# Batch 0's rows in 32-partition transfers, transposes between the units ahead of it, and part of its projections and FFN moved into it

## The chip, the cores and the metric

The kernel is written in Bass for one Trainium2 chip and runs on one of its cores. A core has five engines with instruction streams of their own: TensorE (PE in the profile, with its weight loads as PEld), VectorE (DVE), ScalarE (ACT), GpSimd (POOL) and SyncE (SP), which only starts transfers here. Transfers are issued from SP, from ScalarE's queue (ACTq) and from GpSimd's queue (POOLq), and are carried out by 16 DMA engines. The metric is the time of one execution on the device in microseconds (us); less is better.

## The reference, cut to what matters

x is [16, 512, 128] in fp32: 16 batches of 512 tokens. Wq and Wk are [128, 128] (16 heads of 8), Wv is [128, 1024] (16 heads of 64), Wo is [1024, 128], and the three FFN weights are [128, 128].

```python
xn = (x - mean(x)) / sqrt(var(x) + 1e-5)            # over the last axis
# causal attention, 16 heads, d_k = 8, d_v = 64
q, k, v = heads(xn @ Wq), heads(xn @ Wk), heads(xn @ Wv)
scores = einsum('bhqd,bhkd->bhqk', q, k) / sqrt(8)
attn = softmax(where(causal, -inf, scores))
a = concat_heads(einsum('bhqk,bhkd->bhqd', attn, v)) @ Wo
# FFN on the same xn; prev is xn one token earlier (zeros for the first)
xr = mu_r * xn + (1 - mu_r) * prev
xk = mu_k * xn + (1 - mu_k) * prev
f = sigmoid(xr @ W_r.T) * (square(relu(xk @ W_k.T)) @ W_v.T)
out = x + a + f
```

## The kernel before, in words

**Rows of q and k.** q and k are kept in fp32, each split into a rounded high half and the rest (hi and lo), so that a product of short depth (8 dimensions, as hi, lo, hi of k against hi and lo of q, in 32 rows, with a row or more for statistics behind them) gives fp32 accuracy. project_qk makes the product for all heads with tokens in the free dimension, VectorE splits it (qh and ql, kh and kl), and the halves are written to DRAM: two blocks of 256 KB for q, three for k (hi, lo, hi). spread_qk reads them back in the layout of the matmuls: head pair p (two heads, u = 0 and 1, on partitions from 64u on) holds 32 rows of 512 elements of 2 KB each. One spread fills 16 partitions for several pairs: m = 0 or 1 chooses the lower or the upper 16 of the 32. make_qk reserves the tiles and fills the constant rows by GpSimd's transfers (k<-fill, q<-fill); batch b uses tile b % 2.

**Units.** The attention of one batch is cut into four groups of two head pairs, and each group into UNITS = 5 units, 20 units per batch (`per`), 320 in all, which are counted on through the batches as n. A group's rows go through two passes. In the row pass, rowscores puts q·k (tile sm) into PSUM, rowmask adds the mask, rowmax takes the negative row maximum on VectorE, and rowsum takes the exponential on ScalarE with the sum accumulated. After a group's five units the logarithm of the sums is subtracted from the maximum, transposed (turn_stats) and written into q's rows 33 and 34 by two GpSimd transfers per half (put_stats: q<-mh and q<-ml). In the second pass, scores makes the transposed product (tile sT) with these rows, weights takes its exponential (tile e), and weigh multiplies with v (tile av). The row pass of unit n + 11 is issued with the second pass of unit n: LEAD = 10 units are finished ahead. Units −11 to −1 therefore hold only row work, and are called the lead here; unit 0 issues the first scores.

**What else stands in a unit.** `at(n, f, ...)` puts a piece of other work into unit n, for the same batch or for the next two: layer norm (row_moments, deviation, normalise, transpose_xn), project_qk, spread_qk, project_v (eight products pv per batch of two matmuls each, each followed by a copy into v), mix_prev and mix, and the FFN: ffn_r (product pr) and ffn_exp (e_sig), ffn_sig (reciprocals), ffn_k (product pk), ffn_out (product pkv), then project_out (product po), and load_x. In a unit, unit_work's order is put_stats, rowscores, scores, rowmask, rowmax, rowsum, weights, the pieces, weigh, turn_stats. In unit_work and its pieces every engine keeps the order in which the program is written (the wrapper `_InOrder`, whose line is L44 in the profile: nearly all instructions show that line and are told apart by their tiles). Plain `nc.` calls, as in load_x, are not held to it.

**PSUM.** There are two sm tiles of two banks (ps_sm), one sT tile of two (ps_st), one bank for av (ps_av) and one for everything else (ps_m). m_tile gives out the last one; as long as the list `lent` is not empty (until n = −1) it rotates over ps_m, ps_av and ps_st, which nothing else uses yet.

**Before unit −11.** The program loads x of batches 0 and 1 on SP, the weights Wq, Wk, Wv, the three FFN weights and Wo on ScalarE's queue, sets up constants on GpSimd, normalises batch 0, projects its q (halves written from SP) and k (from ScalarE's queue), builds the mask operands (wide, id2, mask2), spreads pairs 0 and 1 (k on ScalarE's queue, q on SP), then pairs 2 and 3 (SP), transposes the FFN weights (wt), and normalises and projects q of batch 1. Pairs 4 to 7 are spread in units −8 to −5. All eight pv of batch 0 stand in units −10 to −1, pr in −2 and e_sig in −1:

```python
    for m, n in enumerate((0, 2, 3, 4, 5, 6, 7, 9)):
        at(first + n, project_v, 0, m // 2, m % 2)   # first = -LEAD
    at(first + 8, ffn_r, 0)
    at(first + 9, ffn_exp, 0)
    for c, n in enumerate((1, 2, 3, 3)):
        at(n, ffn_sig, 0, c)
    at(2, ffn_k, 0)
    at(4, ffn_out, 0)
```

Of the kernel before, what the change touches and what calls it, by code (L numbers as in the profile page):

```python
# [9 lines left out]
FP = mybir.dt.float32  # L10
# [7 lines left out]
P = 128  # L18
H = 16
DK = 8  # L20
DV = 64
NPAIR = H // 2
RS = 33
RA = 35
UNITS = 5
LEAD = 10
# [23 lines left out]
def attn_ffn_kernel(  # L50
# [27 lines left out]
    nc = tc.nc  # L78
    B, T, D = x.shape
    NB = T // P  # L80
    scale = 1.0 / math.sqrt(DK)

    const = ctx.enter_context(tc.tile_pool(name="const", bufs=1))
# [3 lines left out]
    one = ctx.enter_context(tc.tile_pool(name="one", bufs=1))  # L87
# [3 lines left out]
    dram = ctx.enter_context(tc.tile_pool(name="dram", bufs=2, space=bass.MemoryType.DRAM))  # L91
    ps_sm = ctx.enter_context(tc.tile_pool(name="ps_sm", bufs=2, space=PSUM))
    ps_st = ctx.enter_context(tc.tile_pool(name="ps_st", bufs=1, space=PSUM))
# [5 lines left out]
    pe, dve, act = _InOrder(tc, nc.tensor), _InOrder(tc, nc.vector), _InOrder(tc, nc.scalar)  # L99
    pool, sp = _InOrder(tc, nc.gpsimd), _InOrder(tc, nc.sync)  # L100
# [3 lines left out]
    def load_x(b):  # L104
        xs[b] = xp.tile([P, NB, D], FP, tag="x", name=f"x_{b}")
        nc.sync.dma_start(out=xs[b], in_=x[b].rearrange("(c p) d -> p c d", p=P))
# [4 lines left out]
    for name, w in (("wq", Wq), ("wk", Wk)):  # L111
        t = one.tile([P, H * DK], FP, tag=f"{name}_n", name=f"{name}_n")
# [1 line left out]
        wqk_n.append(t)  # L114
    wv = const.tile([P, H * DV], FP, tag="wv", name="wv")
    nc.scalar.dma_start(out=wv, in_=Wv)
    ffn_n = []
    for i, w in enumerate((W_r, W_k, W_v)):
        t = one.tile([P, D], FP, tag=f"ffn_n{i}", name=f"ffn_n{i}")
        nc.scalar.dma_start(out=t, in_=w)  # L120
        ffn_n.append(t)
    wo = const.tile([P, NPAIR, D], FP, tag="wo", name="wo")
    nc.scalar.dma_start(out=wo, in_=Wo.rearrange("(m p) d -> p m d", p=P))
    if B > 1:
        load_x(1)
    mus = const.tile([P, 2], FP, tag="mus", name="mus")
# [23 lines left out]
    lent = [0]  # L150

    def m_tile(name):
        n = lent[0] % 3 if lent else 0
        if lent:
            lent[0] += 1
        if n == 1:
            return ps_av.tile([P, T], FP, tag="av", name=name)
        if n == 2:
            return ps_st.tile([P, 2, 512], FP, tag="sT", name=name)[:, 0, :]
        return ps_m.tile([P, 512], FP, tag="m", name=name)  # L160

    xnTs, vs, ctxs, ffns, xmix = {}, {}, {}, {}, {}

# [18 lines left out]
    def row_moments(b, c):  # L182
        if c == 0:
            xs[b, "st"] = small.tile([P, NB, 6], FP, tag="st", name=f"st_{b}")
        dve.bn_stats(xs[b, "st"][:, c, :], xs[b][:, c, :])

    def deviation(b):
        st = xs.pop((b, "st"))
        mv = small.tile([P, NB, 2], FP, tag="mv", name=f"mv_{b}")
        for c in range(NB):  # L190
            dve.bn_aggr(mv[:, c, :], st[:, c, :])
        ve = small.tile([P, NB], FP, tag="ve", name=f"ve_{b}")
        dve.tensor_scalar(ve, mv[:, :, 1], EPS, None, ALU.add)
        rstd = small.tile([P, NB], FP, tag="rstd", name=f"rstd_{b}")
        pool.tensor_tensor(rstd, ve, neg_half, ALU.pow)
        xs[b, "mv"] = mv, rstd

    def normalise(b, c, engine=pool):
        if c == 0:
            xs[b, "n"] = small.tile([P, NB, D], FP, tag="xn", name=f"xn_{b}")  # L200
        mv, rstd = xs[b, "mv"]
        engine.tensor_scalar(
            xs[b, "n"][:, c, :], xs[b][:, c, :], mv[:, c, 0:1], rstd[:, c : c + 1],
            ALU.subtract, ALU.mult,
        )

    def transpose_xn(b):
        xn = xs.pop((b, "n"))
        pt = m_tile(f"xnTp_{b}")
        for c in range(NB):  # L210
            pe.transpose(pt[:, c * P : (c + 1) * P], xn[:, c, :], ident)

        xnT = big.tile([P, T + 1], FP, tag="xnT", name=f"xnT_{b}")
        pool.memset(xnT[:, 0:1], 0.0)
        dve.tensor_copy(xnT[:, 1 : T + 1], pt)
        xnTs[b] = xnT

    def project_qk(b, is_k, queue=sp):

        w, name = (wk, "k") if is_k else (wq, "q")  # L220
        pq = m_tile(f"p{name}_{b}")
        product(pq, w, xnTs[b][:, 1 : T + 1])
        hi = one.tile([P, T], FR, tag=f"{name}h", name=f"{name}h_{b}")
        lo = one.tile([P, T], FR, tag=f"{name}l", name=f"{name}l_{b}")
        dve.tensor_copy(hi, pq)
        dve.tensor_tensor(lo, pq, hi.bitcast(FP), ALU.subtract)

        blocks = (hi, lo, hi) if is_k else (hi, lo)
        d = dram.tile([len(blocks), P, T], FP, tag=name, name=f"{name}_{b}")
        for n, half in enumerate(blocks):  # L230
            queue.dma_start(out=d[n], in_=half.bitcast(FP))
        halves[b, name] = d.rearrange("n (d p u) t -> u (n d) p t", u=2, d=DK)

    def spread_qk(b, is_k, m, u, pairs, queue=sp):

        to, name = ((ks if is_k else qs)[b % 2].bitcast(FP), "k" if is_k else "q")
        first = DK * m if is_k else 0
        queue.dma_start(
            out=to[64 * u + 16 * m : 64 * u + 16 * m + 16, pairs],
            in_=halves[b, name][u][first : first + 16, pairs],  # L240
        )

    SPREAD = [(is_k, m, u) for m in range(2) for is_k in (False, True) for u in range(2)]

    def project_v(b, j, i):
        if j == 0 and i == 0:
            vs[b] = big.tile([P, NB, H * DV], FP, tag="v", name=f"v_{b}")
        pv = m_tile(f"pv_{b}_{j}_{i}")
        product(pv, xnTs[b][:, 1 + j * P : 1 + (j + 1) * P], wv[:, i * 512 : (i + 1) * 512])
        dve.tensor_copy(vs[b][:, j, i * 512 : (i + 1) * 512], pv)  # L250

    def mix_prev(b, i):
        prev = one.tile([P, T], FP, tag="prev", name=f"prev_{b}_{i}")
# [75 lines left out]

    def rowscores(b, g, t):  # L330
        q, k = qs[b % 2], ks[b % 2]
        sm = sms[b, g, t] = ps_sm.tile([P, 2, 512], FP, tag="sm", name=f"sm_{b}_{g}_{t}")
        for w, i, to in ROWS[t]:
            n = (i + 1) * P
            for u in range(2):
                s = slice(64 * u, 64 * u + RS)

                pe.matmul(
                    sm[:, u, to : to + n], q[s, 2 * g + w, i * P : n], k[s, 2 * g + w, :n],
                    start=(to == 0), stop=False,  # L340
                )
# [148 lines left out]
    def at(n, f, *args):  # L490
        todo.setdefault(n, []).append((f, args))
# [86 lines left out]
    def make_qk(i):  # L578
        q = const.tile([P, NPAIR, T], FR, tag=f"q{i}", name=f"q{i}")
        k = const.tile([P, NPAIR, T], FR, tag=f"k{i}", name=f"k{i}")  # L580
        for u in range(2):
            r = 64 * u + 32
            for to, value, n in ((q, 0, 1), (k, 1, 3)):
                pool.dma_start(
                    out=to[r : r + n].bitcast(FP),
                    in_=fill[0:n, value : value + 1, :].to_broadcast([n, NPAIR, T]),
                )
        qs.append(q)
        ks.append(k)


    make_qk(0)
    for c in range(NB):
        row_moments(0, c)
    deviation(0)
    for c in range(NB):
        normalise(0, c, dve)
    transpose_xn(0)
    project_qk(0, False)
    project_qk(0, True, act)  # L600

# [17 lines left out]
            dve.tensor_copy(to[half], wide[half, i, P * u : P * u + P])  # L621

    make_qk(1)
    for pairs in (slice(0, 2), slice(2, 4)):
        for is_k, m, u in SPREAD:
            spread_qk(0, is_k, m, u, pairs, act if is_k and pairs.stop == 2 else sp)

    ffn_w = const.tile([P, 3, D], FP, tag="ffn_w", name="ffn_w")
    wt = m_tile("wt")
    for i in range(3):  # L630
        pe.transpose(wt[:, i * D : (i + 1) * D], ffn_n[i], ident)
    dve.tensor_copy(ffn_w.rearrange("p i d -> p (i d)"), wt[:, 0 : 3 * D])


    omm = const.tile([P, 2], FP, tag="omm", name="omm")
    dve.tensor_scalar(omm, mus, -1.0, 1.0, ALU.mult, ALU.add)
    load_x(2)
    for c in range(NB):
        row_moments(1, c)
    deviation(1)  # L640
    for c in range(NB):
        normalise(1, c, dve)
    transpose_xn(1)
    project_qk(1, False)
    first = -LEAD
    at(first + 1, project_qk, 1, True)
    for m, part in enumerate(SPREAD):
        at(first + 2 + m // 2, spread_qk, 0, *part, slice(4, NPAIR))
    for m, n in enumerate((0, 2, 3, 4, 5, 6, 7, 9)):
        at(first + n, project_v, 0, m // 2, m % 2)  # L650
    for i in range(2):
        at(first - 1 + 5 * i, mix_prev, 0, i)
        at(first + 1 + 6 * i, mix, 0, i)
    at(first + 8, ffn_r, 0)
    at(first + 9, ffn_exp, 0)
    for c, n in enumerate((1, 2, 3, 3)):
        at(n, ffn_sig, 0, c)
    at(2, ffn_k, 0)
    at(4, ffn_out, 0)
    at(1, mix_prev, 1, 0)  # L660
    at(5, mix, 1, 0)
    for n in range(first - 1, B * per + 2):
# [38 lines left out]
```

## Time and profile before

| | us |
|---|---|
| median of 3 runs | 1011.81 (1010.26 to 1013.88) |
| profiled execution, in all | 1015.34 |
| its span, first to last instruction | 1013.6 |
| PE busy | 949.4 (94%) |
| ACT busy | 921.6 (91%) |
| DVE busy | 790.4 (78%) |
| POOL busy | 512.4 (51%) |
| mean granted TensorE clock | 0.975 |
| first row exponential (ACT sm) | 29.43 |
| first scores product (PE sT), unit 0 | 57.46 |
| first sT of batch 1 | 123.07 |

The profile is one execution, taken by the hardware profiler. Its page cuts the span into 40 slices of 25.3 us and shows the busy share of each engine in tenths, and the granted clock of TensorE (PEclk; 9 is 90% or more of full speed). Answers of the trace give the same for stretches of any length, single instructions with the idle time before them and what ended it, the sums of such waits, the chain of work that ended last, followed back from its end, and the transfers with the time from issue to landing. In the slices the first four differ from the rest: lower clock, and ScalarE starting late. A busy PE is not PE at full speed: the same product of two to four matmuls takes twice as long at a granted clock of 0.5.

### The profile page before, as it was taken

How to read it: one execution, taken by the hardware profiler on the slowest of the kernel's cores; microseconds unless marked ns; L12 is line 12 of the kernel's file. 1: busy time of each engine (PE TensorE's matmuls, PEld its weight loads, DVE VectorE, ACT ScalarE, POOL GpSimd, SP SyncE). 2: the span in 40 equal slices, each digit the busy share in tenths (PEclk: the TensorE clock that was granted, in tenths of full speed). 3: DMA queues.
4: the chain of work that ended last, by engine and by line, in shares of the span. 5: the costliest groups of instructions: out<-in, count | busy, mean ns of one | idle time of the engine just before them, and what ended most of it. 6: DMA issues, size and time to landing. Idle time of an engine off the chain costs nothing.

```text
span 1013.6 us, 22825 instructions
## 1 busy us (share of the span) xinstructions
PE 949.4 (94%) x8131; PEld 524.4 (52%) x8131; DVE 790.4 (78%) x1312; ACT 921.6 (91%) x2449; POOL 512.4 (51%) x959
## 2 busy tenths in 40 slices
PE   3888999999999999999999999999999999999997
PEld 1244464555546455554645555464555646455454
DVE  4777878787887878788787878878787887877641
ACT  0688999999999999999999999999999999999982
POOL 4146364554646455454645555464465546434431
PEclk8578999999999999999999999999999999999999
DMA  8730513535142353514235341423534131343000
GB/s 183 134 45 13 110 19 70 91 70 91 34 101 28 70 91 70 90 34 99 31 70 90 70 91 34 96 34 70 90 71 81 33 95 25 70 80 49 3 13 11
DMA packets 59968, 67.10 MB, mean 66 GB/s; under 512 B 12928, under 2 KB 33024, under 8 KB 59856
## 3 DMA queue, kind: packets, MB, share of 16 engines
q1 hardware_dynamic: 48688, 61.89, 32.4%
q10 hardware_dynamic: 2528, 2.43, 1.0%
q0 software_dynamic: 8640, 1.34, 1.0%
q8 instruction: 65, 1.06, 0.5%
q14 instruction: 47, 0.39, 0.1%
HBM read 39.13 MB, written 25.17 MB: 63 GB/s over the span
## 4 chain that ended last, share of the span: by engine, by line
ACT 55%; PE 27%; issue 8%; DVE 7%; DMA 2%; POOL 1%; ACTq 0%; POOLq 0%
ACT sm L44 37%; ACT e L44 17%; PE av L44 9%; PE po L44 5%; DVE negm L44 4%; PE sm L44 4%; PE pv L44 3%; PE sT L44 3%; PE xnTp L44 1%; PE pr L44 1%; DVE xnT L44 1%; DMA q<-ml 1%; DVE v L44 1%; DMA k<-k 1%; PE pk L44 1%
## 5 line engine op out<-in xcount | busy, mean ns | idle before, releaser
L44 ACT ACTIVATE sm<-sm,negm 128x384 f32<-128x384 f32 (+3 forms) x1024 | 513.0, 501 | 64.9 <-DMA k<-k 27.3
L44 DVE TENSOR_REDUCE negm<-sm 128x2 f32<-128x768 f32 (+3 forms) x448 | 397.9, 912 | 101.3 <-PE sm L44 99.2
L44 POOL TENSOR_SCALAR_AFFINE_SELECT e<-e 128x256 f32<-128x256 f32 x512 | 200.5, 410 | 432.4 <-ACT e L44 432.3
L44 PE MATMUL av<-e,v 128*64 128x512 f32 (+3 forms) x2048 | 336.5, 438 | 2.4 <-DVE ctx L44 2.4
L44 ACT ACTIVATE e<-sT 128x1024 f32<-128x1024 f32 x320 | 324.1, 1013 | 14.1 <-PE sT L44 14.1
L44 PEld LDWEIGHTS av<-e,v 128*64 128x64 f32 x2048 | 139.7, 137 | 161.6 <-issue 129.6
L44 ACT ACTIVATION_READ_ACCUMULATOR sm<-sm,negm 128x1 f32 x1024 | 200.5, 196 | 0.0
L44 PE MATMUL sm<-k,q 33*128 33x384 f32 (+3 forms) x1024 | 164.8, 378 | 7.4 <-ACT sm L44 5.4
L44 PE MATMUL sT<-q,k 35*128 35x512 f32 (+3 forms) x1024 | 147.7, 335 | 16.5 <-ACT e L44 13.0
L44 PEld LDWEIGHTS sm<-k,q 33*128 33x128 f32 x1024 | 83.6, 188 | 151.8 <-ACT e L44 82.0
L44 PE MATMUL pv<-wv,xnT 128*64 128x512 f32 x512 | 142.3, 633 | 12.6 <-DVE kl L44 5.8
L44 PE MATMUL po<-wo,ctx 128*64 128x128 f32 x2048 | 133.2, 277 | 2.9 <-DVE ctx L44 1.6
L44 PEld LDWEIGHTS po<-wo,ctx 128*64 128x64 f32 x2048 | 109.8, 137 | 15.4 <-DVE v L44 2.6
L44 PEld LDWEIGHTS sT<-q,k 35*128 35x128 f32 x1024 | 91.2, 187 | 45.9 <-ACT e L44 40.0
L44 DVE COPY v<-pv 128x512 f32<-128x512 f32 x128 | 87.6, 684 | 23.2 <-PE pv L44 19.7
L44 DVE COPY ctx<-av 128x512 f32<-128x512 f32 x128 | 87.1, 680 | 12.7 <-PE av L44 12.6
L44 PE MATMUL sm<-mask,id 64*128 64x256 bf16 (+1 forms) x640 | 91.0, 265 | 0.0
L44 POOL DMA_DIRECT2D q<-mh x128 | 69.8, 548 | 24.9 <-DVE mh L44 12.8
L44 POOL DMA_DIRECT2D q<-ml x128 | 65.8, 519 | 0.0
L44 DVE RECIPROCAL sig<-e_sig 128x128 f32<-128x128 f32 x64 | 60.1, 940 | 0.0
L44 POOL TENSOR_SCALAR prev<-xnT,omm 128x512 f32<-128x512 f32 x32 | 50.0, 1564 | 16.2 <-DVE xmix L44 16.2
L44 PEld LDWEIGHTS <-id 64*128 64x128 bf16 x640 | 36.3, 95 | 24.8 <-issue 10.5
(63 smaller groups left out, 571.1 us busy)
## 6 DMA issues: line engine op xcount, KB each, us to landing
q<-q SPq DMA_DIRECT2D x124, 128.0 KB, 4.9
k<-k SPq DMA_DIRECT2D x124, 128.0 KB, 4.7
k<-kh SPq DMA_DIRECT2D x30, 256.0 KB, 2.6
x<-in_L_attn_x_dram SPq DMA_DIRECT2D x16, 256.0 KB, 6.5
q<-qh SPq DMA_DIRECT2D x16, 256.0 KB, 2.0
q<-ql SPq DMA_DIRECT2D x16, 256.0 KB, 2.1
out_dram<-o SPq DMA_DIRECT2D x16, 256.0 KB, 2.8
k<-kl SPq DMA_DIRECT2D x15, 256.0 KB, 2.0
```

Source lines behind the costliest of these rows:

```text
L44: return self._tc.keep_in_program_order(f(*args, **kwargs))
```

## The change

The diff does these things.

- **Halves of k.** The high half of k is written to its two blocks in DRAM by one transfer with a repeated source, instead of two.
- **Spreads of batch 0, pairs 0 to 3.** spread_pair replaces spread_qk there: each transfer fills 32 partitions of one pair (64 KB) where it filled 16 partitions of two pairs (64 KB). The source is walked as two blocks of 16 rows: for q the same 16 rows twice (step 0), for k the second block 8 rows further on. The order is pair by pair; k of pairs 0 and 1 is on ScalarE's queue, the rest on SP.
- **Loads.** The three FFN weights are loaded from SP behind these spreads, and Wo from SP; both were on ScalarE's queue at the start.
- **Third row tile.** Row units 2, 5 and 8 of batch 0 use the ps_st tile; m_tile rotates over two places, not three.
- **TensorE kept busy.** keep_awake(n) issues n transposes of the identity into a spare tile: 32 at the start, 4 behind the transposes of xn, 8 in each of the units −9 to −1.
- **Moved work.** The first half of v's products (pv with i = 0) stands ahead of the spreads, with copies on ScalarE; the second half (i = 1) in units 0, 1, 2 and 4. pr moves from unit −2 to 2, e_sig from −1 to 3, the reciprocals from units 1, 2, 3, 3 to 4, 5, 6, 6, pk from 2 to 4, pkv from 4 to 8. The transposes of the FFN weights move into unit −7, project_qk(1, q) into unit −11, the layer norm of batch 1 ahead of the mask operands.

```diff
@@ -114,13 +114,6 @@
     nc.scalar.dma_start(out=wv, in_=Wv)
-    ffn_n = []
-    for i, w in enumerate((W_r, W_k, W_v)):
-        t = one.tile([P, D], FP, tag=f"ffn_n{i}", name=f"ffn_n{i}")
-        nc.scalar.dma_start(out=t, in_=w)
-        ffn_n.append(t)
-    wo = const.tile([P, NPAIR, D], FP, tag="wo", name="wo")
-    nc.scalar.dma_start(out=wo, in_=Wo.rearrange("(m p) d -> p m d", p=P))
     if B > 1:
@@ -150,14 +143,18 @@
     def m_tile(name):
-        n = lent[0] % 3 if lent else 0
+        n = lent[0] % 2 if lent else 0
         if lent:
...
             return ps_av.tile([P, T], FP, tag="av", name=name)
-        if n == 2:
-            return ps_st.tile([P, 2, 512], FP, tag="sT", name=name)[:, 0, :]
         return ps_m.tile([P, 512], FP, tag="m", name=name)
+    def keep_awake(n):
+        pt = m_tile("awake")
+        for c in range(n):
+            pe.transpose(pt[:, (c % NB) * P : (c % NB + 1) * P], ident, ident)
@@ -225,10 +222,15 @@
-        blocks = (hi, lo, hi) if is_k else (hi, lo)
-        d = dram.tile([len(blocks), P, T], FP, tag=name, name=f"{name}_{b}")
-        for n, half in enumerate(blocks):
-            queue.dma_start(out=d[n], in_=half.bitcast(FP))
+        d = dram.tile([3 if is_k else 2, P, T], FP, tag=name, name=f"{name}_{b}")
+        if is_k:
+            queue.dma_start(
+                out=d[0::2].rearrange("n p t -> p n t"),
+                in_=hi.bitcast(FP)[:, None, :].to_broadcast([P, 2, T]),
+            )
+        else:
+            queue.dma_start(out=d[0], in_=hi.bitcast(FP))
+        queue.dma_start(out=d[1], in_=lo.bitcast(FP))
         halves[b, name] = d.rearrange("n (d p u) t -> u (n d) p t", u=2, d=DK)
@@ -240,14 +242,24 @@
+    def spread_pair(b, is_k, u, p, queue=sp):
+        to, name = ((ks if is_k else qs)[b % 2].bitcast(FP), "k" if is_k else "q")
+        rows = halves[b, name][u][:, p]
+        rows = bass.AP(
+            tensor=rows.tensor, offset=rows.offset,
+            ap=[[rows.ap[0][0] * DK if is_k else 0, 2], [rows.ap[0][0], 2 * DK], *rows.ap[1:]],
+        )
+        queue.dma_start(out=to[64 * u : 64 * u + 32, p], in_=rows)
     SPREAD = [(is_k, m, u) for m in range(2) for is_k in (False, True) for u in range(2)]
...
-    def project_v(b, j, i):
+    def project_v(b, j, i, copy=dve.tensor_copy):
         if j == 0 and i == 0:
...
         product(pv, xnTs[b][:, 1 + j * P : 1 + (j + 1) * P], wv[:, i * 512 : (i + 1) * 512])
-        dve.tensor_copy(vs[b][:, j, i * 512 : (i + 1) * 512], pv)
+        copy(vs[b][:, j, i * 512 : (i + 1) * 512], pv)
@@ -329,7 +341,10 @@
         q, k = qs[b % 2], ks[b % 2]
-        sm = sms[b, g, t] = ps_sm.tile([P, 2, 512], FP, tag="sm", name=f"sm_{b}_{g}_{t}")
+        n = UNITS * g + t
+        space, tag = (ps_st, "sT") if b == 0 and n < LEAD and n % 3 == 2 else (ps_sm, "sm")
+        sm = sms[b, g, t] = space.tile([P, 2, 512], FP, tag=tag, name=f"sm_{b}_{g}_{t}")
         for w, i, to in ROWS[t]:
@@ -590,14 +605,34 @@
     make_qk(0)
+    keep_awake(32)
     for c in range(NB):
...
     transpose_xn(0)
+    keep_awake(4)
     project_qk(0, False)
     project_qk(0, True, act)
+    for j in range(3):
+        project_v(0, j, 0, act.copy)
+    for p in range(4):
+        for u in range(2):
+            for is_k in (False, True):
+                spread_pair(0, is_k, u, p, act if is_k and p < 2 else sp)
+    ffn_n = []
+    for i, w in enumerate((W_r, W_k, W_v)):
+        t = one.tile([P, D], FP, tag=f"ffn_n{i}", name=f"ffn_n{i}")
+        sp.dma_start(out=t, in_=w)
+        ffn_n.append(t)
+    project_v(0, 3, 0, act.copy)
+    for c in range(NB):
+        row_moments(1, c)
+    deviation(1)
+    for c in range(NB):
+        normalise(1, c, dve)
+    transpose_xn(1)
@@ -621,42 +656,43 @@
     make_qk(1)
-    for pairs in (slice(0, 2), slice(2, 4)):
-        for is_k, m, u in SPREAD:
-            spread_qk(0, is_k, m, u, pairs, act if is_k and pairs.stop == 2 else sp)
-    ffn_w = const.tile([P, 3, D], FP, tag="ffn_w", name="ffn_w")
-    wt = m_tile("wt")
-    for i in range(3):
-        pe.transpose(wt[:, i * D : (i + 1) * D], ffn_n[i], ident)
-    dve.tensor_copy(ffn_w.rearrange("p i d -> p (i d)"), wt[:, 0 : 3 * D])
...
     dve.tensor_scalar(omm, mus, -1.0, 1.0, ALU.mult, ALU.add)
-    load_x(2)
-    for c in range(NB):
-        row_moments(1, c)
-    deviation(1)
-    for c in range(NB):
-        normalise(1, c, dve)
-    transpose_xn(1)
-    project_qk(1, False)
+    ffn_w = const.tile([P, 3, D], FP, tag="ffn_w", name="ffn_w")
+    wo = const.tile([P, NPAIR, D], FP, tag="wo", name="wo")
+    def turn_ffn():
+        wt = m_tile("wt")
+        for i in range(3):
+            pe.transpose(wt[:, i * D : (i + 1) * D], ffn_n[i], ident)
+        dve.tensor_copy(ffn_w.rearrange("p i d -> p (i d)"), wt[:, 0 : 3 * D])
+    def load_wo():
+        sp.dma_start(out=wo, in_=Wo.rearrange("(m p) d -> p m d", p=P))
     first = -LEAD
+    at(first - 1, project_qk, 1, False)
     at(first + 1, project_qk, 1, True)
+    at(first + 6, load_x, 2)
+    at(first + 7, load_wo)
     for m, part in enumerate(SPREAD):
         at(first + 2 + m // 2, spread_qk, 0, *part, slice(4, NPAIR))
-    for m, n in enumerate((0, 2, 3, 4, 5, 6, 7, 9)):
-        at(first + n, project_v, 0, m // 2, m % 2)
+    for n in range(1, LEAD):
+        at(first + n, keep_awake, 8)
+    at(first + 3, turn_ffn)
     for i in range(2):
-        at(first - 1 + 5 * i, mix_prev, 0, i)
-        at(first + 1 + 6 * i, mix, 0, i)
-    at(first + 8, ffn_r, 0)
-    at(first + 9, ffn_exp, 0)
-    for c, n in enumerate((1, 2, 3, 3)):
+        at(first + 2 + 2 * i, mix_prev, 0, i)
+        at(first + 3 + 2 * i, mix, 0, i)
+    for j, n in enumerate((0, 1, 2, 4)):
+        at(n, project_v, 0, j, 1)
+    at(2, ffn_r, 0)
+    at(3, ffn_exp, 0)
+    for c, n in enumerate((4, 5, 6, 6)):
         at(n, ffn_sig, 0, c)
-    at(2, ffn_k, 0)
-    at(4, ffn_out, 0)
+    at(4, ffn_k, 0)
+    at(8, ffn_out, 0)
     at(1, mix_prev, 1, 0)
```

## The prediction

> **What bounds the kernel now.** I read the times and the page's slices first, then windows of the stages that the change touches, then chain, waits, DMA and single rows of the first 60 us. The profiled execution spans 1013.6 us and took 1015.34 in all, 3.5 above the median of 1011.81; sums are made on 1015.34 and then lowered by 3.5. About ±0.3% (3 us) is what this kernel's measurement tells from no change.
>
> The page's engine totals and its clock slices:
>
> ```profile
> PE   3888999999999999999999999999999999999997
> ACT  0688999999999999999999999999999999999982
> PEclk8578999999999999999999999999999999999999
> ```
>
> Only the first four slices (101 us) are loose. Windows (us; busy us of TensorE, its weight loads, VectorE, ScalarE, GpSimd, each with its count; granted clock; DMA share; GB/s):
>
> ```profile
> 16.00:18.00 2.00, 0.00 (x0) 0.00 (x0) 1.90 (x12) 0.00 (x0) 0.00 (x0) 0.77 0.94 327
> 36.00:48.00 12.00, 12.00 (x43) 3.62 (x39) 9.56 (x15) 8.45 (x29) 2.33 (x3) 0.51 1.03 175
> 48.00:58.00 10.00, 6.48 (x49) 2.99 (x45) 7.56 (x12) 8.42 (x29) 2.89 (x4) 1.00 1.10 134
> 57.50:73.10 15.60, 14.34 (x83) 6.94 (x83) 11.64 (x19) 13.27 (x34) 7.30 (x13) 0.67 0.12 16
> 88.00:96.00 8.00, 6.81 (x23) 2.53 (x25) 2.94 (x6) 6.38 (x19) 1.28 (x4) 0.57 0.01 3
> 183.00:243.00 60.00, 58.31 (x523) 33.11 (x524) 49.65 (x82) 58.00 (x156) 32.45 (x61) 1.00 0.39 70
> ```
>
> In the steady state TensorE and ScalarE are both full at full clock, and the change leaves it alone. What it can win lies between the start and 123.07 us, where batch 1's first sT product starts. Chain and waits:
>
> ```profile
> 15.41 4.88 DMA k<-kl
> 21.62 5.02 DMA k<-k
> 26.66 2.77 DMA k<-k
> ...
> ACT sm L44 <- DMA k<-k: 27.3, 1, 27.3
> PE sT L44 <- DMA q<-ml: 1.5, 1, 1.5
> ```
>
> The row exponentials start at 29.43, after the rows of k, and the first sT at 57.46: 28.03 us for ScalarE work of 22.9 (10.3 per group of five units by the ACT rows, two groups, 2.3 for unit 10). The half clock fills TensorE there (12.00 of 12.00 at 0.51). Batch 0 then takes 65.6 us against 58.8 for a steady batch.
>
> **First rows (prologue).** The three FFN weights (192 KB) leave ScalarE's queue ahead of the halves: 0.6 us at 327 GB/s; Wo and x of batches 2 and 3 still stand ahead on SP. The projection ahead of them takes 1.97 us at half clock:
>
> ```profile
> 10.35 1.97 PE L44 MATMUL pq<-xnT,wq 128*64 128x512 f32 x4 [0.79 <-DVE xnT L44]
> 13.84 0.55 PE L44 MATMUL wt<-ident,ffn_n 128*128 128x128 f32 x3
> 35.54 1.97 PE L44 MATMUL pv<-wv,xnT 128*64 128x512 f32 x4
> 53.67 1.08 PE L44 MATMUL pv<-wv,xnT 128*64 128x512 f32 x4 [0.27 <-DVE e_sig L44]
> ```
>
> at 1.08 if the 32 new transposes warm it. So q's halves, landed at 20.05 before, land near 18.5. On ScalarE's queue the four k spreads stand behind three v copies: from 14.0, three pv of 1.9 and a copy of 0.69 give 20.4, where the first k spread left at 20.31. Without those copies it could leave about 1.2 earlier; that is what the added wait costs. Taking v's copies off VectorE there is free: ScalarE waits for rows anyway. GpSimd's deviation of batch 1 (1.05) now precedes the mask work and make_qk(1)'s four issues (0.6 each); before, all this was done by 19.2, masks are first needed at 26: nothing, at worst +1. VectorE now normalises and turns batch 1 before it casts the masks; it was 5.0 of 10 us busy from 20 to 30, so the casts still come before 26: 0. q of batch 1 is projected in unit −11 instead of ahead of it, on a TensorE that then waits for rows: 0, at worst its two products, +2 warm or +4 cold, if rows came earlier.
>
> **The spreads, the unknown price.** Before, 16 transfers of 64 KB (16 partitions × 2 pairs) land 0.5 to 0.6 us apart, 22.4 to 29.7. After: again 16 of 64 KB, now 32 partitions × 1 pair, and the source is walked as two blocks of 16 rows. No row shows that form.
>
> ```profile
> q<-q SPq DMA_DIRECT2D x8, 64.0 KB, 4.0
> k<-k ACTq DMA_DIRECT2D x4, 64.0 KB, 3.8
> ...
> k<-fill POOLq DMA_DIRECT2D x4, 48.0 KB, 7.4
> ```
>
> Low end 0.3 us each: twice as fast as now, were partitions the limit. High end: the window at 16:18 moves 327 GB/s over 16 DMA engines, 20 GB/s each, or 94 ns per 2-KB row; 32 rows over two engines, one per source block, are 16 × 94 = 1.5 us. I take 1.5: of the rows above, k<-fill, whose outermost step is also small (3), is nearest in form and slowest per byte, though GpSimd's queue differs. Both ends stay for the range.
>
> The Trainium skill's "DMA: Bandwidth & Descriptors", in "Rules for kernel authors" and its account of how many engines a transfer gets, has the number of engines as the largest up to 16 that divides both patterns' slowest dimension; by it these transfers get two engines, 24 us in all, where the old ones got 16. "SBUF — State Buffer", in its section on the port swizzle, has 32 partitions nearly twice as fast as 16, which would halve the old 0.55 instead. No row here decides between them.
>
> At 1.5 each, 16 take 24 us: 18.5 to 42.5. Pair 0 is whole four transfers after 20.4, at 26.4; first exponential 2.77 later (as 26.66 to 29.43), 29.2: −0.2. Pairs 1 to 3 follow every 6 us, in time for ScalarE at two units of 2.06 per pair and one for both.
>
> **Rest of the lead.** Out of it go eight pv (four into the prologue, four into batch 0), pr and e_sig (0.61 of ScalarE, now in unit 3); in come nine times eight transposes. Transposes were 0.21 us apart cold (four between 8.3 and 9.1), 0.11 warm: 1.7 or 0.87 us per unit. With sm and mask (0.92 cold, 0.55 warm) TensorE needs 2.62 or 1.42 per unit; ScalarE needs 2.06. The third row tile only helps where TensorE is ahead: its worth is inside the 5.1 us of lead that is not ScalarE work. turn_ffn stands in unit −7, ahead of row unit 5, and waits for weights now queued behind SP's spreads: 42.5 + 0.8 = 43.3. TensorE gets there at 39 to 41, and everything behind it waits: wt's 0.6, then six units of 2.62 make the first sT 59.6 against 57.46: **+2.1** cold. Warm, ScalarE leads again: 57.5, **0**. The eight 128-KB spreads of pairs 4 to 7 and batch 1's 13 (1.03 us each before) start later on SP; the q<-ml transfer waits among them, as it did (8.96 us in the chain), within a us of that time.
>
> **Batch 0.** Units 0 to 4 held 12.2 us of TensorE work at full clock. Four pv (1.08) and pr (1.09) come in, pkv (1.09) goes to unit 8: 16.6. From unit −1 on all share one PSUM bank, so in units 0, 2 and 4 a second product waits 0.69 for a VectorE copy: 2.0. VectorE gains 3.5 on 11.64 of 15.6 and keeps up. Before, the clock was half until 68.3; with 8 us at half clock, 16.6 + 4, and half of the waits beside ScalarE's work anyway, 21.1 against 15.6: **+5.5** (warm +1 to +3). The dip at 88.8 to 95.6, where TensorE idles for ScalarE (units 10 to 14: 17.8 against 14.7 steady), may go as TensorE lags: **−2.5** (0 to −4).
>
> k's high half written twice by one transfer: one issue less per batch on an SP queue with room; if 512 KB take twice the 2.6 us of 256, the next spreads of k are three units (8.8 us) away: 0. Earlier x of batch 2, later Wo (needed in unit 22): 0.
>
> Sum, cold: +2.1 + 5.5 − 2.5 = +5.1 → 1020.4 profiled, **1017** against the median.
>
> **Will the transposes hold the clock?** 36:48 shows TensorE busy throughout and yet at 0.51, so being busy by these records does not buy the clock; 48:58 has 1.00 at 65% busy, after several pv. I take the cold lead.
>
> "TensorE: Matmul & The Clock Gate", in its part on PE-mode transposes, says that a transpose does not count as busy for the clock in the same way. By that rule the 72 transposes only cost their time (cold lead, 1017); were it wrong here, 1012.
>
> **Rivals.**
> 1. Slow spreads, warm clock: 0 + 2 − 2 = 0 → 1012 (1009 to 1015). For it: wt at 13.84 ran three transposes in 0.55, at full clock. Against: 36:48.
> 2. The other side: spreads at 0.6 or less. Then pair 0 is there at 22, the first exponential at 24.8, the FFN weights at about 29, before unit −7 needs them, and ScalarE's 22.9 set the lead: first sT near 49.5, −8. Warm, +2 − 2.5 behind it: −8.5 → 1003, at best −12 → 1000. It decides from about 0.9 us per spread, where the weights come in time. For it: twice as many partitions per transfer and the old 0.55. Against: the two-step outer walk.
> 3. The change does not do what it says: fast spreads, but the transposes do not warm the clock. TensorE's 11 × 2.62 = 28.8 from 22.5 set the lead, first sT 52.3: −5 + 5.5 − 2.5 = −2 → 1010.
>
> **How the numbers follow.** Cold and slow spreads 0.48 (1017, own range 1012 to 1023; 120 ns per row would give 1023): slower 0.40, same 0.05, faster 0.03. Rival 1, 0.20: 0.06 faster, 0.08 same, 0.06 slower. Rival 2, 0.22, all but 0.01 faster. Rival 3, 0.10: 0.07 faster, 0.01 same, 0.02 slower. Together faster 0.37, same 0.15, slower 0.48. The range leaves out the better half of rival 2 and the tail above 1023: 1001 to 1023.
>
> **What would show it.** In the profile after: q<-q and k<-k of 64 KB landing 1.5 us apart and the last near 42; TensorE waiting at wt for ffn_n; a granted clock of 0.5 from 17 to 48; the first sT near 59.6; units 0 to 4 near 21 us; no dip near 90. The prediction falls if spreads land 0.6 apart, if the clock stays at 1.0 from 20 on, or if batch 0 hides the moved products behind ScalarE.

## The result and the profile after

The changed kernel takes 1021.55 us (median of 4 runs, 1020.38 to 1023.06) against 1012.24 for the kernel before: a ratio of 1.0094, interval 1.0069 to 1.0118. The forecast was slower, 1017, with a range up to 1023. The profiled execution took 1022.49 (span 1020.8), 7.15 more than that of before. Executions of one kernel differ too: those of before beside the last experiments took 1009.71 to 1015.86 at mean granted clocks of 0.973 to 0.995, so the marks of one profiled execution and a median can disagree by a few us.

The engine and clock slices of the page of the changed kernel:

```profile
PE   5878999999999999999999999999999999999997
...
ACT  1668899999999999999999999999999999999982
...
PEclk8769999999999999999999999999999999999999
```

Windows of the same kernel, with columns as before (us; busy us and count of TensorE, its weight loads, VectorE, ScalarE, GpSimd; granted clock; DMA share; GB/s):

```profile
20.00:30.00 10.00, 2.03 (x8) 1.22 (x10) 0.33 (x1) 0.58 (x1) 2.02 (x2) 0.50 0.25 59
...
36.00:48.00 12.00, 11.91 (x82) 8.82 (x80) 9.00 (x15) 8.87 (x30) 1.77 (x2) 0.83 0.83 208
48.00:58.00 10.00, 5.82 (x43) 4.12 (x41) 4.74 (x7) 9.30 (x33) 1.92 (x4) 0.96 1.09 141
57.50:73.10 15.60, 13.87 (x57) 5.93 (x57) 7.46 (x12) 8.43 (x21) 5.56 (x10) 0.50 0.25 34
88.00:96.00 8.00, 6.04 (x64) 3.44 (x60) 7.23 (x10) 7.11 (x20) 5.45 (x10) 1.00 0.01 1
183.00:243.00 60.00, 58.28 (x518) 32.88 (x516) 49.66 (x83) 58.03 (x156) 32.37 (x61) 1.00 0.36 69
```

The steady state is the same. From 20 to 30 nearly everything stands still although the DMA engines are used only to a quarter. The lead's second half is warmer than before (0.83 against 0.51), but 57.5 to 73.1 lies wholly at half clock, where before had 0.67.

Where the 7.15 us are can be read from the starts of the exponentials e, one per unit, in the two traces:

| us | before | after | difference |
|---|---|---|---|
| first row exponential | 29.41 | 31.06 | +1.7 |
| e of unit 0 | 58.39 | 58.87 | +0.5 |
| units 0 to 4, e to e | 17.29 | 23.09 | +5.8 |
| units 5 to 9 | 16.40 | 17.58 | +1.2 |
| units 10 to 14 | 17.80 | 16.89 | −0.9 |
| units 15 to 19 | 15.28 | 15.29 | 0 |
| first e of batch 1 | 125.16 | 131.71 | +6.6 |

From there to the end the two differ by 0.6 more. The chain of the changed kernel's start, and its waits in the first 75 us (total, times, longest, in us):

```profile
17.46 5.61 DMA q<-q
...
23.09 10.63 DMA k<-k
...
48.88 8.62 DMA q<-ml
```

```profile
PE sm L44 <- DMA k<-k: 11.0, 3, 8.1
...
ACT v L44 <- DMA q<-q: 7.2, 1, 7.2
...
PEld pr L44 <- DVE v L44: 2.5, 1, 2.5
PEld pm L44 <- DVE v L44: 2.5, 1, 2.5
...
PE sT L44 <- DMA q<-ml: 1.9, 1, 1.9
```

TensorE waits longer for k's rows. By the chain ScalarE's last spread leaves at 23.09, only when a transfer q<-q has landed. In batch 0 products queue behind the copies of v. The first row exponential scatters by itself: it lies between 30.21 and 31.45 in the three kernels that are the same up to there with the new spreads (after, a_moved_back, a_warm), and between 25.84 and 27.60 in the six with the old ones. The transfers alone, changed kernel, 30 to 36 us, in 40 slices (busy share of the DMA engines in tenths, and GB/s):

```profile
DMA  1111111111111111111127341111111114653863
GB/s 55 41 55 41 55 55 41 55 41 55 55 55 41 55 41 55 55 55 41 41 92 246 113 133 58 41 55 55 55 41 41 55 55 130 195 185 103 188 198 106
```

While only spreads are under way they move about 51 GB/s at a tenth of the engines' time: 1.28 us for 64 KB. Before, in the stretch of the spreads from 23 to 29 us:

```profile
DMA  9999999899999979999998999999999899999899
...
DMA packets 593, 0.84 MB, mean 140 GB/s; under 512 B 182, under 2 KB 182, under 8 KB 593
```

That is 140 GB/s at nine tenths: 0.47 us for 64 KB.

### The profile page after: what moved, and what is told of

Read it like the earlier page. It is cut to its first block, busy times and chain, and to the rows that moved or that the text cites. A ratio compares the mean times of both kernels' runs of the same rounds, so it can differ in the third digit from the quotient of the medians.

```text
span 1020.8 us, 23032 instructions
## 1 busy us (share of the span) xinstructions
PE 958.6 (94%) x8239; PEld 537.5 (53%) x8239; DVE 786.7 (77%) x1308; ACT 924.4 (91%) x2453; POOL 513.7 (50%) x959
## 3 DMA queue, kind: packets, MB, share of 16 engines
q8 instruction: 66, 1.08, 0.5%
## 4 chain that ended last, share of the span: by engine, by line
ACT 58%; PE 24%; issue 8%; DVE 6%; DMA 3%; POOL 0%; SPq 0%; ACTq 0%
ACT sm L44 39%; ACT e L44 18%; PE av L44 7%; PE po L44 4%; DVE negm L44 3%; PE sm L44 3%; PE pv L44 3%; PE sT L44 3%; PE xnTp L44 1%; DMA k<-k 1%; DVE xnT L44 1%; DMA q<-ml 1%; PE pr L44 1%; DVE v L44 1%; ACT e_sig L44 1%
## 5 line engine op out<-in xcount | busy, mean ns | idle before, releaser
L44 ACT ACTIVATE e<-sT 128x1024 f32<-128x1024 f32 x320 | 324.2, 1013 | 20.1 <-PE sT L44 19.7
L44 PE MATMUL pv<-wv,xnT 128*64 128x512 f32 x512 | 139.7, 624 | 12.5 <-DVE kl L44 6.1
L44 DVE COPY v<-pv 128x512 f32<-128x512 f32 x124 | 84.9, 685 | 22.5 <-PE pv L44 19.2
```

Of the source, the lines that this page charges most:

```text
L44: return self._tc.keep_in_program_order(f(*args, **kwargs))
```

## The experiments

Two theories went in. A: two separate costs, the new spreads' in the lead, the moved products' in batch 0. B: the spreads cause all of it, since late statistics leave TensorE idle and it then runs batch 0 at half clock. All runs in one table; times of stages are from the profiled execution, medians and ratios to the kernel before from the runs beside it.

| run | first row exp. | e of unit 0 | units 0–4 | first e of batch 1 | median | ratio (interval) |
|---|---|---|---|---|---|---|
| before | 29.41 | 58.39 | 17.29 | 125.16 | | 1 |
| after | 31.06 | 58.87 | 23.09 | 131.71 | 1021.55 | 1.0094 (1.0069 to 1.0118) |
| a_old_spreads | 25.84 | 50.40 | 23.11 | 123.49 | 1015.74 | 1.0042 (1.0023 to 1.0061) |
| b_new_spreads | 32.83 | 60.69 | 16.77 | 126.85 | 1016.81 | 1.0043 (1.0027 to 1.0059) |
| a_moved_back | 30.21 | 58.99 | 16.41 | 123.98 | 1015.45 | 1.0028 (1.0018 to 1.0038) |
| a_no_awake | 31.70 | 57.56 | 22.35 | 131.25 | 1021.24 | 1.0088 (1.0072 to 1.0104) |
| c_both_back | 27.60 | 53.89 | 18.06 | 121.10 | 1009.74 | 0.9970 (0.9952 to 0.9989) |
| a_warm | 31.45 | 60.91 | 17.53 | 128.23 | 1016.45 | 1.0032 (1.0015 to 1.0050) |
| a_old_warm | 26.41 | 50.93 | 22.22 | 122.85 | 1011.83 | 0.9985 (0.9959 to 1.0010) |
| a_half_columns | 32.10 | 58.70 | 24.89 | 134.51 | 1024.75, one run | |
| c_v_warm | 26.72 | 51.91 | 21.45 | 122.69 | 1013.80 | 1.0015 (1.0001 to 1.0029) |
| c_both_warm | 27.39 | 55.38 | 17.99 | 122.64 | 1012.34 | 0.9992 (0.9977 to 1.0008) |
| a_old_warm2 | 27.05 | 53.71 | 24.09 | 128.77 | 1010.62 | 1.0004 (0.9972 to 1.0036) |
| a_pair16 | 24.79 | 51.80 | 22.31 | 123.80 | 1013.77, one run | |

**Old spreads in the changed kernel.**

```diff
-    for p in range(4):
-        for u in range(2):
-            for is_k in (False, True):
-                spread_pair(0, is_k, u, p, act if is_k and p < 2 else sp)
+    for pairs in (slice(0, 2), slice(2, 4)):
+        for is_k, m, u in SPREAD:
+            spread_qk(0, is_k, m, u, pairs, act if is_k and pairs.stop == 2 else sp)
```

> The changed kernel, but pairs 0 to 3 are spread as before: 16 transfers of 16 partitions and two pairs, in the old order and on the old queues. Marks of the changed kernel's profile: first row exponential 31.06, exponential e of unit 0 at 58.87, of unit 5 at 81.96, median 1021.6. Theory A (the spreads on two DMA engines cost the lead alone, and the moved products cost batch 0): spreads land 0.5 to 0.6 us apart, the first row exponential comes at 26 to 28, e of unit 0 at 54 to 57, but units 0 to 4 still take 21 to 23 us; 1016 to 1020. Rival B (the slow spreads cause all of it: they push back the row statistics of unit 0, TensorE idles and falls to half clock in batch 0): e of unit 0 at 50 to 53, units 0 to 4 in 16 to 18 us, 1006 to 1010.

e of unit 0 comes at 50.40, 8.5 us earlier than in the changed kernel and 8.0 earlier than before: as B said. Units 0 to 4 still take 23.11: as A said. So in this kernel the spreads set the lead and change nothing in batch 0. The marks stand ahead of those of before and the median behind it: this profiled execution took 2.0 us less than its median, that of before 3.1 more than its own. Windows of this run, to be held against 20:30 above:

```profile
20.00:30.00 10.00, 7.24 (x25) 2.72 (x26) 4.88 (x7) 3.27 (x11) 2.10 (x2) 0.58 0.57 133
50.40:73.50 23.10, 20.05 (x102) 8.62 (x103) 14.34 (x29) 15.26 (x39) 9.91 (x16) 0.66 0.12 16
```

**New spreads in the kernel before.** The reverse of that diff, with the helper.

> The kernel before, with pairs 0 to 3 spread in 16 transfers of 32 partitions and one pair, in pair order; nothing else of the change. Marks of before: first row exponential 29.41, e of unit 0 at 58.39, of unit 5 at 75.67, median 1012.2. Theory A: 1.3 us per spread, first row exponential near 31, e of unit 0 at 59 to 61, units 0 to 4 as before in 17 to 18 us: 1013 to 1015. Rival B: the row statistics land late, and batch 0 runs longer at half clock: 1018 or more.

The first row exponential is 3.4 us later and e of unit 0 2.3 later, batch 0 is unchanged (16.77). The ratio, 1.0043, is above the +1.7 us that the marks of the profiled executions show. A was right on the place, but the median, 1016.81, lies between A's 1013 to 1015 and B's 1018.

**Moved products back in the changed kernel.**

```diff
-    for j, n in enumerate((0, 1, 2, 4)):
-        at(n, project_v, 0, j, 1)
-    at(2, ffn_r, 0)
-    at(3, ffn_exp, 0)
-    for c, n in enumerate((4, 5, 6, 6)):
+    for j, n in enumerate((2, 4, 6, 9)):
+        at(first + n, project_v, 0, j, 1)
+    at(first + 8, ffn_r, 0)
+    at(first + 9, ffn_exp, 0)
+    for c, n in enumerate((1, 2, 3, 3)):
         at(n, ffn_sig, 0, c)
-    at(4, ffn_k, 0)
-    at(8, ffn_out, 0)
+    at(2, ffn_k, 0)
+    at(4, ffn_out, 0)
```

> The changed kernel, with what it moved into batch 0 back in the lead: second half of v's products in units -8, -6, -4 and -1, FFN products and reciprocals at their old places. Spreads, transposes and third row tile stay as changed. Theory A: units 0 to 4 in 16 to 18 us instead of 23; e of unit 0 by 0 to 3 us later than 58.87, since TensorE takes 5.4 us more at full clock in a lead that waits for rows and statistics anyway; 1015 to 1018. Rival B: units 0 to 4 still take over 20 us because the clock is half there; 1020 to 1023.

Units 0 to 4 fall to 16.41 and e of unit 0 stays (58.99): A. In a lead that waits for rows and statistics the moved work costs nothing. The half-clock stretch shrank along with it, from 17.06 us to 6.83 (60.20 to 67.03), so this run alone does not part the work from the clock.

**Without the transposes.**

```diff
-    keep_awake(32)
-    keep_awake(4)
-    for n in range(1, LEAD):
-        at(first + n, keep_awake, 8)
```

> The changed kernel without its 108 transposes of the identity. Their clock: with them 1.0 from 6.05 to 19.7 and from 40.18 to 57.25. If the transposes warm the clock, it is half in most of both stretches here, pq takes 1.97 instead of 1.08, and q's halves land 0.9 later. Theory A (the lead is set by transfers and ScalarE): first row exponential 31 to 32.5, e of unit 0 at 58 to 60, units 0 to 4 in 22 to 24 us, 1020 to 1024. Rival C (the transposes are what TensorE needs in the lead): e of unit 0 at 62 or later, 1025 or more. Rival D (the transposes only stand in the way): e of unit 0 before 57, 1018 or less.

The clock is 0.5 from 23.53 to 71.32, where the changed kernel had 1.0 from 40.18 to 57.25: the transposes do raise it. e of unit 0 is 1.3 us earlier all the same, and the time is that of the changed kernel: a warm clock buys nothing in a lead that waits for transfers. (A had 58 to 60 for this e, D before 57; 57.56 lies between.) Here TensorE did wait for the late FFN weights:

```profile
40.72 0.90 PE L44 MATMUL wt<-ident,ffn_n 128*128 128x128 f32 x3 [1.81 <-DMA ffn_n<-in_L_ffn_W_r_dram]
```

**Both undone.** The first and the third diff together.

> The changed kernel with both undone: pairs 0 to 3 spread as before, and the moved products back in the lead. Left of the change are the first half of v's products ahead of the spreads, the order of loads, the transposes, the third row tile, the doubled write of k's high half. So far: old spreads alone took 8.5 us from e of unit 0 (58.87 to 50.40), moving back alone took units 0 to 4 from 23.1 to 16.4. Theory A (two costs that add up): e of unit 0 at 50 to 52, units 0 to 4 in 16 to 17 us, first e of batch 1 near 116 against 125.2 before; 1003 to 1008. Rival E (they share one cause, so that the second undoing wins nothing): e of unit 0 back at 55 or later, since TensorE's 5.4 us of moved work is in the shorter lead's way; 1010 or more.

It is the one version measured to be faster than before, by 0.3%. By the medians the two undoings add up, as far as intervals of about ±0.002 tell: the ratio falls by 0.0052 with the old spreads alone, by 0.0066 with the products moved back alone, and by 0.0124 with both. The marks do not show it (e of unit 0 at 53.89 and not at 50.40, units 0 to 4 in 18.06), but this profiled execution was the slowest of its ten, 2.4 us above the median. Of the 3.5 us between 50.40 and 53.89, 1.8 lie already in the first row exponential, ahead of any moved product; what is left, 1.7, is what the moved products can have cost in this lead. The time lies between the ranges of A (1003 to 1008) and E (1010 or more); A's range was too low: the two single steps, 5.8 and 6.1 us off 1021.55, already give 1009.6.

**The clock held into batch 0.** The changed kernel, with TensorE given transposes where it sat idle at the end of the lead:

```diff
-        at(first + n, keep_awake, 8)
+        at(first + n, keep_awake, 8 if n < LEAD - 1 else 24)
...
             rowscores(*stat_next)
+        if n == 0:
+            keep_awake(16)
```

> The changed kernel with more transposes of the identity at the end of the lead, where TensorE sat idle and the granted clock fell to a half at 57.25: 24 instead of 8 in unit -1, and 16 between the row product and the scores of unit 0. Nothing else. If the cold clock is what makes the moved work dear (units 0 to 4 hold 15.4 us of TensorE time at full clock, worked out from 23.1 less half of the 15.4 us at half clock; without the transposes 22.35 less half of 13.8 gives 15.5): the clock holds past 58, e of unit 0 stays at 58 to 59, units 0 to 4 in 15.5 to 18 us, 1014 to 1017. If the cost is the wait for the shared PSUM bank and VectorE's copies, or the clock falls anyway: units 0 to 4 still 22 to 24 us, 1020 to 1023.

The clock stays at 1.0 from 43.37 to 94.57, and units 0 to 4 take 17.53 with the moved products in them; the median falls by 5.1 us. e of unit 0 is 2.0 later than without the added transposes. Units 0 to 4, e to e, of before, of the changed kernel and of this run:

```profile
58.40:75.70 17.30, 15.20 (x90) 7.42 (x91) 14.21 (x28) 14.58 (x40) 9.36 (x16) 0.71 0.06 7
```

```profile
58.90:82.00 23.10, 20.06 (x102) 8.66 (x103) 14.38 (x29) 15.24 (x40) 9.99 (x16) 0.67 0.11 15
```

```profile
60.90:78.50 17.60, 13.82 (x102) 6.21 (x103) 14.11 (x29) 15.26 (x40) 9.95 (x16) 1.00 0.11 15
```

The same 102 matmuls of the last two take 20.06 us at 0.67 and 13.82 at 1.00. In the second TensorE sets the pace; in the third ScalarE's 15.26 lies above it. Here the moved work is dear because it falls into a cold stretch: at full clock units 0 to 4 take 0.2 us more than in the kernel before at its 0.71.

**The same with the old spreads**, with 24 and 6 transposes, and again with 24 and 16:

> The changed kernel with the old spreads and more transposes at the end of the lead (24 in unit -1, 6 between the row product and the scores of unit 0). Without them this kernel had e of unit 0 at 50.40, half clock from 48.93 to 66.0 and units 0 to 4 in 23.1 us. If warmth decides: e of unit 0 at 50 to 51, units 0 to 4 in 15.5 to 18 us, 1004 to 1009, as good as the kernel with the products moved back. If the moved work costs by itself: units 0 to 4 over 20 us, 1012 to 1016.

> The changed kernel with old spreads and 24 and 16 transposes at the lead's end, 10 more than in the run where the clock fell at 51.29 in the profiled execution and where the runs split into 1007.9 to 1010.1 at a mean clock of 0.991 to 0.993 and 1013.5 to 1017.4 at 0.980 to 0.986. If the clock is what splits them: the clock holds in most runs, units 0 to 4 in 16 to 18 us, 1006 to 1010. If not, the split stays.

Neither settles at the warm time. The runs split by the granted clock: in the first 1007.9 to 1010.1 at a mean of 0.991 to 0.993, five others 1013.5 to 1017.4 at 0.980 to 0.986; in the second six runs 1007.6 to 1010.9 at 0.989 and more, four 1016.8 to 1019.7 at 0.980 to 0.982. Both profiled executions fell into the cold part (clock lost at 51.29 and 55.20). More transposes did not remove the split, and nothing here shows what decides it.

**Products instead of transposes.**

```diff
-        for c in range(n):
-            pe.transpose(pt[:, (c % NB) * P : (c % NB + 1) * P], ident, ident)
+        for c in range(n // 2):
+            product(pt[:, (c % NB) * P : (c % NB + 1) * P], ident, ident)
```

> The changed kernel with its transposes of the identity replaced by ordinary products of the identity with itself, each pair of them on 64 columns of TensorE, as the kernel's own products are; by the trace two of them take the time of two transposes (0.49 us at half clock). It asks what raises the clock. If any busy TensorE does, the clock goes to 1.0 near 40 as with the transposes. If it is the share of the array in use, 64 columns are too few: half clock through the lead, as without the transposes, and e of unit 0 at 60 to 64 since TensorE now needs 2.6 us per unit.

The clock rises at 40.47, as with the transposes at 40.18. Rows of this run, and then of the changed kernel (start, us, instruction):

```profile
37.47 1.92 PE L44 MATMUL awake<-ident 128*64 128x128 f32 x16
...
40.18 1.21 PE L44 MATMUL awake<-ident 128*64 128x128 f32 x16
...
41.88 1.09 PE L44 MATMUL awake<-ident 128*64 128x128 f32 x16
```

```profile
36.64 1.97 PE L44 MATMUL awake<-ident 128*128 128x128 f32 x8
...
39.39 1.45 PE L44 MATMUL awake<-ident 128*128 128x128 f32 x8
...
41.34 1.09 PE L44 MATMUL awake<-ident 128*128 128x128 f32 x8
42.27 0.49 PE L44 MATMUL wt<-ident,ffn_n 128*128 128x128 f32 x3
```

In this one run half the columns did as well, so it was not the share of columns in use that raised the clock.

**A version put together**: old spreads, FFN back in the lead, v's second half in batch 0, 24 and 16 transposes.

> A version put together from the runs: old spreads, the FFN back in the lead, the second half of v's products in units 0, 1, 2 and 4 as changed, and the clock held by 24 transposes in unit -1 and 16 between the row product and the scores of unit 0. From the runs: e of unit 0 at 50 to 52 (50.40 with old spreads), units 0 to 4 in 15.5 to 18 us if the clock holds, units 5 to 9 in 16.4 (without pkv), first e of batch 1 at 115 to 119: 1003 to 1008. If the clock falls all the same: units 0 to 4 over 20 us, 1009 to 1013.

The clock held, from 31.37 to 68.92, and yet units 0 to 4 took 21.45. So a cold clock is not the only price: pkv stood in unit 4 right behind the last pv, for the same PSUM bank, and all of TensorE's queue waited with it for VectorE, which had two reciprocals of 0.9 us and a row maximum ahead of the copy of v:

```profile
69.01 1.98 PE L44 MATMUL pkv<-ffn_w,kr 128*64 128x128 f32 x16 [3.11 <-DVE v L44]
```

**Both undone, and the clock**, with 16 transposes ahead of the first scores of c_both_back.

> Old spreads, moved products back in the lead, and 16 transposes between the row product and the scores of unit 0, where the same kernel without them lost the clock at 53.6. That kernel had e of unit 0 at 53.89, units 0 to 4 in 18.06, 5 to 9 in 16.30, 10 to 14 in 17.54. If holding the clock is worth what it was in the changed kernel: units 0 to 4 in 15 to 16.5, 1005 to 1008. If ScalarE sets batch 0 here whatever the clock: units 0 to 4 in 17 to 18, 1008 to 1011.

The clock fell at 58.69 instead of 53.6, units 0 to 4 stayed at 17.99, and the transposes delayed the first e to 55.38. Nothing won.

**Pairs of 16 partitions.**

```diff
-        rows = halves[b, name][u][:, p]
-        rows = bass.AP(...)
-        queue.dma_start(out=to[64 * u : 64 * u + 32, p], in_=rows)
+        for m in range(2):
+            r = DK * m if is_k else 0
+            queue.dma_start(
+                out=to[64 * u + 16 * m : 64 * u + 16 * m + 16, p],
+                in_=halves[b, name][u][r : r + 16, p],
+            )
```

> The changed kernel, with every 32-partition transfer of a pair cut into two of 16 partitions (32 KB each), still in pair order and on the same queues: only the form of the transfers differs. If the two-step walk of the source keeps them on two DMA engines, all 16 carry these: DMA share near 0.5 or more instead of 0.10 to 0.13, over 100 GB/s instead of 51, first row exponential at 24 to 27, e of unit 0 at 49 to 52, as with the old spreads. If the pair order or the queues were to blame: first row exponential at 29 to 31, e of unit 0 at 57 to 59.

Twice the transfers of half the size in the same order: the first row exponential comes at 24.79, the earliest of all, and e of unit 0 at 51.80. The stretch from 16 to 24 us:

```profile
16.00:24.00 8.00, 3.21 (x14) 1.30 (x10) 4.10 (x12) 0.58 (x1) 6.05 (x13) 0.85 0.52 97
```

A DMA share of 0.52 at 97 GB/s is about what was expected. The form of the transfers was the cost, not the pair order. The edit takes away both the two-step walk and the 32 partitions; that it is the walk follows from the busy share of two engines in 16, and no run tried 32 partitions with another walk.

## Why the prediction was right

- **The bound.** Right: the steady state did not move, and the difference lies ahead of batch 1.
- **The spreads.** The price taken was 1.5 us each, from two engines at 94 ns per row; measured 1.28. The low end, 0.3, did not come, and a_pair16 shows that the form sets the price. The rule of the Trainium skill's "DMA: Bandwidth & Descriptors" ("Rules for kernel authors") agrees: a busy share of 0.10 to 0.13 is two engines of 16. The one from "SBUF — State Buffer" on the port swizzle, 32 partitions nearly twice as fast as 16, did not show at 1.28 us; no run here fills 32 partitions by another walk.
- **First row exponential.** Predicted −0.2, measured +1.7. Pair 0 was not whole after four transfers: TensorE waited for k's rows at 25.99 and again at 28.63. By then SP had issued five q<-q (from 16.02), so transfers of later pairs probably shared the two engines; no run parts this.
- **Rest of the lead.** Predicted +2.1 from a cold TensorE behind late FFN weights; e of unit 0 moved by +0.5. This step failed in its mechanism. The transposes raised the clock at 40.18, and wt ran at 42.27 with no wait; what set the first sT, at 57.64, was the transfer q<-ml (8.62 us in the chain), as before. "Will the transposes hold the clock? I take the cold lead" was wrong, and rival 1's condition came true in the lead. The rule of "TensorE: Matmul & The Clock Gate" on transposes, which spoke for the cold lead, does not hold in these runs: 32 transposes were TensorE's only work before the clock stood at 1.0 from 6.05 on, and pq took 1.08 us, against 1.98 in a_no_awake.
- **Batch 0.** Predicted +5.5, measured +5.8 from e to e, with the mechanism: work for TensorE, doubled by the half clock. a_warm shows it, with the work and a full clock 17.53; a_moved_back, without the work, 16.41. The size was partly luck. The 15.6 that it started from is the time between the first sT of units 0 and 5; in these marks it went from 15.68 (57.46 to 73.14) to 23.79 (57.64 to 81.43), +8.1, because e of unit 5 came 2.5 us after its sT in the kernel before and 0.5 in the changed one. The term that was too small is the half clock: 8 us were taken, it lasted from 57.25 to 74.31. And the terms named add up to 21.6 (16.6 + 4 + half of 2.0), not to 21.1. The full-clock price of +1 to +3 was too high for a_warm (+0.2) and too low for c_v_warm (+4.2), where the waits for the bank were longer. Rival 1 assumed that a clock warm through the lead stays so in batch 0; in the profiled execution it fell just there. Where it was held, in a_warm, the time was 1016.45, above rival 1's 1009 to 1015.
- **Units 5 to 9.** Left at nothing, measured +1.2: pkv's 1.09 was taken out of units 0 to 4 but not added where it went. With the FFN back in its old place these units take 16.30 to 16.45 (a_moved_back, c_both_back, c_v_warm).
- **The dip.** Predicted −2.5, measured −0.9. It did not go; it came later and lasted 3.4 us (98.21 to 101.62) instead of 6.8.
- **Rival 2** had the value of fast spreads right: it put the first sT near 49.5, and a_old_spreads has it at 48.97, e of unit 0 8.0 us before that of the kernel before. But in that lead too the clock was lost before unit 0, so batch 0 ate 5.8 of it.
- **Rival 3.** Its first sT comes by its own terms, 22.5 + 28.8, at 51.3 and not at 52.3. Its condition, fast spreads and a cold lead, did not come: in a_old_spreads 8 transposes took 1.09 us from 32.26 on.
- **The sum.** +0.5 + 5.8 + 1.2 − 0.9 and 0.6 behind batch 0 are +7.15, against +5.1. The other 2.6 us between 1017 and 1021.55 come from the reduction by 3.5: the profiled execution of before lay 3.1 above its median, that of the changed kernel only 0.9. It was luck that the lead, 1.6 too dear in the forecast, hid part of batch 0, which came out 3.1 dearer (5.8 + 1.2 − 0.9 against 5.5 − 2.5).

Put together, the rest of the new prologue and lead, with the moved products out of it, was worth 8.0 us to the start of batch 0; the new spreads took 8.5 of it back, and the products moved into batch 0 cost 5.8 where the clock was half. Two things stay open. The third row tile, the doubled write of k's half, the order of loads and v's first half ahead of the spreads were not tried alone. And why the shorter lead keeps the clock in some executions and not in others is not settled.

## What to carry to other kernels

Look at the outermost steps of both sides of a transfer before its size or its partitions: the same 64 KB took 1.28 us with an outermost step of two (two engines, by the busy share) and 0.47 before, and the bytes per transfer told nothing of it. Work that is moved off a stretch where TensorE has room must be priced at the clock of the place where it lands, and for the place in the queue that it takes there: the same 102 matmuls kept TensorE busy for 13.8 us or for 20.1. A piece taken out of one stage has to be added to the other; and a gain in front of a wait for something else (here the statistics' transfer) is only worth what is left behind that wait.

## What the runs showed of the hardware

Granted clock and busy TensorE are not the same thing. In the changed kernel TensorE was busy 13.87 of 15.60 us from 57.5 on and stayed at 0.50 until 74.31; in the lead 1.0 came at 40.18, 3.5 us after the first group of eight transposes had started (36.64, with a row product behind it), and at 40.47, 3.0 us after sixteen matmuls of 64 columns in their place (37.47). All changes of the clock lie on a grid of 3.41 us (19.70, 40.18, 57.25 and 74.31 in the changed kernel are whole multiples apart), and it fell after stretches like 53.84 to 57.25, in which TensorE ran one row product of 0.49 us. That products against few rows (33 or 35 deep, as sm and sT) count for less than deep ones would fit these rows, but no run tells it apart.

By the busy shares two DMA engines carried 51 GB/s, an estimated 25 each; sixteen carried 140 in the kernel before, an estimated 9 each. Spreading over all engines was worth a factor of 2.7 here and not of 8.
